# Graph attention on one core: keys in 32-partition transfers, and another order of the first loads

## The chip, the cores and the metric

The kernel runs on one core of a Trainium2 chip. The metric is the device time of one execution in microseconds (us). Three runs before the change took 10,980.81 to 10,985.29 us, with a median of 10,982.34 us.

The core has five engines that run side by side, each with its own list of instructions: TensorE (PE; its weight loads are shown as PEld), VectorE (DVE), ScalarE (ACT), GpSimd (POOL) and SyncE (SP). SP and POOL here issue the data transfers (DMA), which 16 DMA engines carry out. The engines wait for one another, and for transfers, by semaphores.

## The reference

The network has four graph layers over 3,327 nodes with 128 features, all with the same dense 3,327 x 3,327 matrix `adj`. Layer 0 is attention and takes nearly all of the time:

```python
q = (x @ Wq.T).reshape(d, n, h)
k = (x @ Wk.T).reshape(d, n, h)
v = (x @ Wv.T).reshape(d, n, h)
a = jnp.einsum('dnh,dmh->dnm', q, k) * scale
a = a + spatial_encoding + edge_encoding
a = jax.nn.softmax(a, axis=2)
out = jnp.einsum('dnm,dmh->dnh', a, v)
out = out.reshape(n, h * d)
return out @ Wo.T
```

Both encodings are `adj`, `d` is 128 and `h` is 8. So there are 128 "heads" of 8 elements each, and for each head a 3,327 x 3,327 matrix of scores, to which 2 adj is added. Layers 1 to 3 multiply `adj` (and once its transpose) with 3,327 x 128 matrices, with small functions of each row between them.

## The kernel before

**Stages.** A first stage (up to about 419 us in the profile) makes q, k and v, writes them to DRAM in a form cut into a high and a low half (`qS_d`, `kS_d`), and makes the first part of the transposed adj (`adjT`) and a bound for each column's scores. The attention loop follows, and then layers 1 to 3 (from about 10,167 us).

**The attention loop.** It runs over 7 chunks `c` of 476 query columns, in each over 32 groups `g` of 4 heads, and in each group over 13 pairs `q` of key tiles (2 x 128 keys): 224 groups, 2,912 pairs. For a pair, VectorE seeds a PSUM bank with adj minus the bound (`seed`, L645). TensorE then adds the scores of head 0, then those of head 1 minus those of head 0, and so on, four times into the same bank (`scores`, L654), and ScalarE takes the exponential after each (`exps`, L666 and L669; some by VectorE, `hand_exp`, L691 to L697). TensorE multiplies the exponentials with the values into one bank (`values`, L713). At the end of a group VectorE copies that bank out (`store`, L721) and POOL issues four transfers to `oT_d` (L725).

**Tiles that the change touches.** `KT[b]` holds a group's keys, [128 partitions, 3 slots, 1664]. `b` alternates from group to group, so one group's keys can be loaded while the group before computes. Partitions 0 to 63 hold even key tiles (`r` = 0), 64 to 127 odd ones. A score matmul contracts over 64 partitions: 32 for one head and 32 for the head before it, with negative q. The 32 partitions of one head hold its 16 rows of keys (8 elements, high and low half) twice. Head `j` stands in slots `max(0, j-1)` to `j` (heads 0 and 3 in one slot, 1 and 2 in two) at partition `r0 = 64 * r + 32 * (1 - j % 2)`. `QS[b]` holds the group's q the same way, [128, 4, 476]; `QZ[b]` is a second q of head 1 with zeros, for the pairs done in part by VectorE. `VA[b]` holds the values, spread from the loaded `VR` by POOL (`spread_v`, L580).

**How keys and q are loaded.** `load_k` (L551) issues, for each head, each `r` and each of the two copies, a transfer of 16 rows into 16 partitions and one or two slots: 16 transfers a group. `load_q` issues, for each `r`, one transfer of 16 rows (L562) and two of 8 rows (L564, the halves exchanged). `negate_q` (L570, POOL) writes minus slot `j` over all 128 partitions of slot `j + 1`, after which `load_q` of head `j + 1` overwrites its own 32 partitions of each half. So the loads and negations of a group form a ladder: q of head 0, negation, q of head 1, negation, q of head 2, negation, q of head 3. `all_here` (L584, POOL) copies three columns of `KT` to `seen`; the first score matmul of a group waits for it, and so for all keys.

**What sets the order.** The instructions are recorded by hand: the function `loads(u)` puts the next group's loads behind fixed pairs of the present one: keys, q of head 0 and V behind pair 1, a negation and the next q behind pairs 3, 5 and 7, spreading V and `all_here` behind pair 8. All these transfers are issued by SP, whose list is carried out in order. SP uses eight completion semaphores in turn, so a transfer also waits until the one eight places before it has landed. Adj tiles of the next chunk (`load_adj`, L590) and rows of adj for the next part of `adjT` (`Square`, L283) stand in the same list.

**The first group** has no group before it. Its loads are written out ahead of the loop:

```python
v0 = load_v(0, 0)
load_k(0, 0)
load_q(0, 0, 0)
shift_of[0] = load_shift(0)
for j in range(3):
    negate_q(0, 0, j)
    load_q(0, 0, j + 1)
spread_v(0, 0, v0)
here[0] = all_here(0, 0)
adj_of[0] = [load_adj(0, t) for t in range(NT)]
```

Of the kernel before, what the change touches and what calls it, by code (L numbers as in the profile page):

```python
# [10 lines left out]
F32 = mybir.dt.float32  # L11
# [6 lines left out]
ALU = mybir.AluOpType  # L18
# [4 lines left out]
P = 128  # L23
N = 3327
D = 128
H = 8
HD = D * H
NT = 26
NP = NT * P
NQ = NT // 2  # L30

KW = NP // 4
HEADS = D
# [3 lines left out]
CW = 476  # L37
# [40 lines left out]
def width_of(c):  # L78

    return min(CW, N + 1 - c * CW)  # L80
# [8 lines left out]
def gnn_kernel(ctx: ExitStack, tc: tile.TileContext, x, adj, Wq, Wk, Wv, Wo, embed, layer,  # L89
               embed_bias, layer_bias, weight, bias, W_in, W_out, out):  # L90
    nc = tc.nc
# [14 lines left out]
    kS_d = dram.tile([2, H, HEADS, NP], F32, name="kS_d")  # L106
# [219 lines left out]
    with tc.tile_pool(name="a1", bufs=1) as a1, tc.tile_pool(name="a2", bufs=2) as a2, \  # L326
# [23 lines left out]
        for t0 in range(0, NT, 2):  # L350
            for s in "kq":
# [3 lines left out]
                for i in range(2):  # L355
                    t = t0 + i
# [16 lines left out]
                for half in range(2) if s == "q" else ():  # L373
                    nc.sync.dma_start(places(qS_d, t0, 2, H, half * H * GP), st[half].bitcast(F32))
                nc.gpsimd.dma_start(bass.AP(tensor=n2_d[s].tensor, offset=n2_d[s].offset + t0 * P,
                                            ap=[[NT * P, P], [1, 2 * P]]), n2.rearrange("p t i -> p (t i)"))
# [63 lines left out]
    with tc.tile_pool(name="d1", bufs=1) as d1, tc.tile_pool(name="d2", bufs=2) as d2, \  # L440
# [17 lines left out]
        with tc.If(loose > 0):  # L458
# [28 lines left out]
            for c in range(NC):  # L487
# [5 lines left out]
                with tc.For_i(0, HEADS, 1) as d:  # L493
# [6 lines left out]
                        tensor=v_d.tensor, offset=v_d.offset,  # L500
                        ap=[[N * H, HEADS], [NT * H, P], [1, NT * H]])[ds(d, 1)].rearrange("a p x -> (a p) x"))
# [23 lines left out]
    with tc.tile_pool(name="e1", bufs=1) as e1, tc.tile_pool(name="e_adj", bufs=28) as e_adj, \  # L525
# [5 lines left out]
        KT = [e1.tile([P, 3, NQ * P], F32R, name=f"KT{i}") for i in range(2)]  # L531
        QS = [e1.tile([P, 4, CW], F32R, name=f"QS{i}") for i in range(2)]
# [8 lines left out]
        def load_k(c, g):  # L541

            b = (c * NG + g) % 2
            for j in range(4):
                d = 4 * g + j
                k0, nk = max(0, j - 1), 1 if j in (0, 3) else 2
                for r in range(2):
                    r0 = 64 * r + 32 * (1 - j % 2)
                    k_d = kS_d[:, :, d, r * NQ * P:(r + 1) * NQ * P].rearrange("i e n -> (i e) n")
                    for i in range(2):  # L550
                        nc.sync.dma_start(KT[b][r0 + 16 * i:r0 + 16 * i + 16, k0:k0 + nk, :].bitcast(F32),  # L551
                                          k_d.unsqueeze(1).to_broadcast([16, nk, NQ * P]))

        def load_q(c, g, j):

            b = (c * NG + g) % 2
            w, c0, d = width_of(c), c * CW, 4 * g + j
            q_d = qS_d[:, :, d * N + c0:d * N + c0 + w].rearrange("i e n -> (i e) n")
            for r in range(2):
                r0 = 64 * r + 32 * (1 - j % 2)  # L560
                for q_s in [QS[b][:, j, :]] + [QZ[b]] * ((r, j) == (1, 1)):
                    nc.sync.dma_start(q_s[r0:r0 + 16, :w].bitcast(F32), q_d)  # L562
                    for i in range(2):
                        nc.sync.dma_start(q_s[r0 + 16 + 8 * i:r0 + 24 + 8 * i, :w].bitcast(F32),  # L564
                                          q_d[8 - 8 * i:16 - 8 * i])

        def negate_q(c, g, j):

            b, w = (c * NG + g) % 2, width_of(c)
            nc.gpsimd.tensor_scalar(QS[b][:, j + 1, :w], QS[b][:, j, :w].bitcast(F32),  # L570
                                    -1.0, 0.0, op0=ALU.mult, op1=ALU.add)

        def load_v(c, g):
            v = e2.tile([P, 4, NT * H], F32, name="VR", bufs=1)
            nc.sync.dma_start(v, bass.AP(tensor=v_d.tensor, offset=v_d.offset + 4 * g * N * H,
                                         ap=[[NT * H, P], [N * H, 4], [1, NT * H]]))
            return v

        def spread_v(c, g, v):
            nc.gpsimd.tensor_copy(VA[(c * NG + g) % 2][:, :, :, 0:H], v.rearrange("p j (t e) -> p t j e", e=H))  # L580

        def all_here(c, g):

            return nc.gpsimd.tensor_copy(seen, KT[(c * NG + g) % 2][:, :, 0].bitcast(F32))  # L584

        def load_adj(c, t):

            a = e_adj.tile([P, CW], F32, name="a")
            w, c0 = width_of(c), c * CW
            nc.sync.dma_start(a[:, :w], by_tile[t, :, c0:c0 + w])  # L590
            return a

        def load_shift(c):
            w = width_of(c)
            s = e2.tile([P, CW], F32, name="shb", bufs=2)
            nc.sync.dma_start(s[:, :w], bound_d[c * CW:c * CW + w].unsqueeze(0).to_broadcast([P, w]))
            return s

        with tc.If(loose < 1), tc.manual_schedule():
# [12 lines left out]
            n = len(pairs)  # L612
            adj_of, shift_of, v_of, e_of, here = {}, {}, {}, {}, {}
# [113 lines left out]
            def loads(u):  # L727

                c, g, q = pairs[u]
                k = c * NG + g  # L730
                if k + 1 < NC * NG:
                    nxt = divmod(k + 1, NG)
                    if q == 1:
                        load_k(*nxt)
                        load_q(*nxt, 0)
                        v_of[k + 1] = load_v(*nxt)
                    if q in (3, 5, 7):
                        negate_q(*nxt, q // 2 - 1)
                        load_q(*nxt, q // 2)
                    if q == 8:  # L740
                        spread_v(*nxt, v_of.pop(k + 1))
                        here[k + 1] = all_here(*nxt)
                if c + 1 < NC and (g, q) == (0, 0):
                    plan_squares(c)
                if g == NG - 1 and c + 1 < NC:
                    if q == 0:
                        shift_of[c + 1] = load_shift(c + 1)
                        adj_of[c + 1] = []
                    while len(adj_of[c + 1]) < min(NT, 2 * q + 6):
                        adj_of[c + 1].append(load_adj(c + 1, len(adj_of[c + 1])))  # L750
# [4 lines left out]
            def plan(u, f, *a):  # L755
                behind.setdefault(u, []).append((f, a))

            def plan_squares(c):
                for k, s in enumerate(range(squares_of(c), squares_of(c + 1))):
# [7 lines left out]
                    for k, f in ((0, sq.gather), (1, sq.back), (7, sq.finish), (8, sq.store)):  # L767
                        plan(u + k, f)

            v0 = load_v(0, 0)  # L770
            load_k(0, 0)
            load_q(0, 0, 0)
            shift_of[0] = load_shift(0)
            for j in range(3):
                negate_q(0, 0, j)
                load_q(0, 0, j + 1)
            spread_v(0, 0, v0)
            here[0] = all_here(0, 0)
            adj_of[0] = [load_adj(0, t) for t in range(NT)]

            for c in range(NC):
                for q in BY_HAND:
# [7 lines left out]
            def in_slot(i):  # L790

                j = -i % 4
                return (i - 3 * j) // 4, j


            for i in range(-4, 4 * n + 15):
                u, j = in_slot(i)
# [21 lines left out]
                if at % 2:  # L819
                    for k in (1, 2):  # L820
                        u, j = in_slot(i + k)
                        if 0 <= u < n:
                            scores(u, j)
                    u, r = ((i - 11) // 4, 0) if at == 3 else ((i - 13) // 4, 1)
# [682 lines left out]
```

## Time and profile before

| | |
|---|---|
| median of three runs | 10,982.34 us |
| profiled execution, its own time | 10,981.96 us |
| its span, first to last instruction | 10,980.2 us |
| mean granted TensorE clock | 0.985 |
| PE busy | 10,533.5 us, 96% |
| ACT busy | 10,033.1 us, 91% |
| DVE busy | 8,487.1 us, 77% |
| POOL busy | 1,529.1 us, 14% |
| moved by DMA | 1,256.98 MB, mean 114 GB/s |
| share of the transfers issued by SP (queue q1) | 55.7% of 16 engines' span |
| first and last score matmul (L654) | 461.1 and 10,166.9 us |

Busy time is that of each engine. Engines overlap, so shares don't add up. In an order of time a line has the start, the duration, the engine, the line of the kernel, the operation and its tiles; "SPq" is SP's issuing of transfers, and its duration is that of the issue, waits between issues included where several are merged, not of the transfer. In brackets stands the idle time before it and what ended it. In a table of stretches each row has a stretch, its length, each engine's busy time with its number of instructions, the granted clock, the share of the 16 DMA engines' time and GB/s.

### The profile page before, as it was taken

To read this page: it belongs to the slowest core of one execution; us is meant where nothing else is said; L and a number is where in the kernel's file an instruction comes from. 1 tells how busy PE (TensorE), PEld (TensorE's weight loads), DVE (VectorE), ACT (ScalarE), POOL (GpSimd) and SP (SyncE) were. 2 spreads that over 40 slices of the span, in tenths; PEclk is the share of its full clock that TensorE was granted. 3 is DMA by queue.
4 is the path that set the end of the run, shared out by engine and by line. 5 is a ranking of instruction groups with operands and counts; after the bars stand their busy time and mean duration, and the time that the engine had idled before them with its cause. 6 is when DMAs were issued, how large, how long until landed. Compare 5 with 4: busy or idle time off the path is not lost. (4 is left out here: it accounts for less than half of the span.)

```text
span 10980.2 us, 204474 instructions
## 1 busy us (share of the span) xinstructions
PE 10533.5 (96%) x72876; PEld 3435.7 (31%) x72876; DVE 8487.1 (77%) x13503; ACT 10033.1 (91%) x13789; POOL 1529.1 (14%) x2477
## 2 busy tenths in 40 slices
PE   4599999999999999999999999999999999999889
PEld 2133333333333333333333333333323333333544
DVE  5588887888878887788887888878877777777655
ACT  3599999999999999999999999999999999999330
POOL 5011111111111111111111111111111111111101
PEclk7799999999999999999999999999999999999999
DMA  8766566565566565565556565565556555554668
GB/s 250 250 99 97 94 96 113 93 98 96 89 118 97 93 97 88 106 98 97 90 95 119 94 96 93 95 119 95 87 93 98 96 95 86 82 88 71 206 233 281
DMA packets 695339, 1256.98 MB, mean 114 GB/s; under 512 B 195218, under 2 KB 555049, under 8 KB 691244
## 3 DMA queue, kind: packets, MB, share of 16 engines
q1 hardware_dynamic: 644044, 1114.42, 55.7%
q0 software_dynamic: 50272, 129.37, 4.3%
q8 instruction: 587, 9.62, 0.4%
q14 instruction: 436, 3.57, 0.2%
HBM read 1096.53 MB, written 146.60 MB: 113 GB/s over the span
## 5 line engine op out<-in xcount | busy, mean ns | idle before, releaser
L666 ACT ACTIVATE e<-S 128x952 f32<-128x952 f32 (+1 forms) x9024 | 8357.9, 1099 | 36.7 <-PE S L654 29.4
L713 PE MATMUL po<-e,VA 128*9 128x476 f32 (+1 forms) x46592 | 5737.5, 564 | 33.0 <-DVE OS L721 12.3
L645 DVE TENSOR_TENSOR S<-a,shb 128x476 f32<-128x476 f32 (+1 forms) x5824 | 3937.9, 676 | 1447.6 <-ACT e L666 1059.4
L654 PE MATMUL S<-QS,KT 64*128 64x476 f32 (+1 forms) x22176 | 4528.6, 445 | 79.7 <-DMA a<-adjT 28.4
L654 PEld LDWEIGHTS S<-QS,KT 64*128 64x128 f32 x22176 | 2073.7, 184 | 5100.5 <-issue 1301.3
L669 ACT ACTIVATE e<-S 128x476 f32<-128x476 f32 (+1 forms) x4128 | 2467.5, 711 | 1.1 <-PE S L654 0.6
L695 DVE SCALAR_TENSOR_TENSOR e<-e,h 128x476 f32<-128x476 f32 (+1 forms) x2240 | 1497.8, 669 | 77.0
L713 PEld LDWEIGHTS po<-e,VA 128*9 128x9 f32 x46592 | 691.0, 88 | 1606.6 <-issue 1488.1
L570 POOL TENSOR_SCALAR QS<-QS 128x476 fp32r<-128x476 f32 (+1 forms) x672 | 485.6, 723 | 4312.1 <-DMA QS<-qS_d 2612.2
L725 POOL DMA_DIRECT2D oT_d<-OS x896 | 470.5, 530 | 3668.8 <-DVE OS L721 3625.5
L691 DVE TENSOR_SCALAR h<-S 128x476 f32<-128x476 f32 (+1 forms) x1120 | 728.0, 650 | 300.9 <-PE S L654 296.5
L697 DVE SCALAR_TENSOR_TENSOR e<-e,EA 128x476 f32<-128x476 f32 (+1 forms) x1120 | 759.6, 678 | 0.0
L695 DVE SCALAR_TENSOR_TENSOR e<-h 128x476 f32<-128x476 f32 (+1 forms) x1120 | 743.1, 663 | 0.0
L1107 PE MATMUL pu<-strip,y 128*128 128x512 f32 (+2 forms) x1456 | 600.5, 566 | 31.7 <-DVE y L968 14.8
L654 PE MATMUL S<-QZ,KT 64*128 64x476 f32 (+1 forms) x1120 | 493.4, 441 | 11.9 <-DVE S L645 10.5
L1107 PEld LDWEIGHTS pu<-strip,y 128*128 128x128 f32 (+1 forms) x1456 | 271.9, 191 | 305.8 <-issue 272.1
L1111 DVE TENSOR_REDUCE deg<-strip 128x1 f32<-128x1536 f32 (+1 forms) x104 | 193.8, 1881 | 63.7 <-DMA strip<-adjT 44.1
L580 POOL COPY VA<-VR 128x832 f32<-128x832 f32 x224 | 242.3, 1082 | 0.0
L654 PEld LDWEIGHTS S<-QZ,KT 64*128 64x128 f32 x1120 | 205.1, 183 | 92.2 <-DVE S L645 52.4
L288 DVE STREAM_TRANSPOSE cols<-rows 128x416 f32<-128x416 f32 x208 | 204.5, 988 | 30.3 <-DMA rows<-in_adj_dram 22.6
L1060 ACT COPY uT<-pu 128x512 f32<-128x512 f32 (+1 forms) x21 | 11.1, 555 | 222.6 <-PE pu L1107 222.6
L721 DVE COPY OS<-po 128x476 f32<-128x476 f32 (+1 forms) x224 | 146.3, 653 | 87.3 <-PE po L713 87.3
(255 smaller groups left out, 1958.6 us busy)
## 6 DMA issues: line engine op xcount, KB each, us to landing
KT<-kS_d SPq DMA_DIRECT2D x1792, 208.0 KB
KT<-kS_d SPq DMA_DIRECT2D x1792, 104.0 KB
VR<-v_d SPq DMA_DIRECT2D x224, 416.0 KB
QS<-qS_d SPq DMA_DIRECT2D x3072, 14.9 KB
QS<-qS_d SPq DMA_DIRECT2D x1536, 29.8 KB
adjT<-cols SPq DMA_DIRECT2D x26, 1664.0 KB
a<-adjT SPq DMA_DIRECT2D x156, 238.0 KB
strip<-adjT POOLq DMA_DIRECT2D x39, 895.5 KB, 5.1
```

Source lines behind the costliest of these rows:

```text
L570: nc.gpsimd.tensor_scalar(QS[b][:, j + 1, :w], QS[b][:, j, :w].bitcast(F32), -1.0, 0.0, op0=ALU.mult, op1=ALU.add)
L580: nc.gpsimd.tensor_copy(VA[(c * NG + g) % 2][:, :, :, 0:H], v.rearrange("p j (t e) -> p t j e", e=H))
L645: touch(u, [r], nc.vector.tensor_tensor(bank(u, r), adj_of[c][2 * q + r][:, :w], shift_of[c][:, :w], op=ALU.subtract))
L654: x = nc.tensor.matmul(bank(u, r), KT[b][64 * r:64 * r + 64, max(0, j - 1), q * P:(q + 1) * P], q_s[64 * r:64 * r + 64, :w], start=hand an ...
L666: touch(u, (0, 1), nc.scalar.activation(e[:, :, :w], S[:, odd:even + 1, :w], AF.Exp, scale=2.0))
L669: touch(u, [r], nc.scalar.activation(e[:, 1 - r, :w], bank(u, r), AF.Exp, scale=2.0))
L691: touch(u, [1], nc.vector.tensor_scalar(s, bank(u, 1), EXP_ARG, None, op0=ALU.mult))
L695: nc.vector.scalar_tensor_tensor(e, s if k == 3 else e, EXP_C[k], s, op0=ALU.add, op1=ALU.mult)
L697: nc.vector.scalar_tensor_tensor(e, e, EXP_C[0], EA[pairs[u][2]][:, :w], op0=ALU.add, op1=ALU.mult)
L713: nc.tensor.matmul(po[32 * j:32 * j + H + 1, :w], VA[k % 2][:, 2 * pairs[v][2] + of, j, :], e_of[v, j][:, 1 - of, :w], start=(q == 0 and r ...
L725: nc.gpsimd.dma_start(oT_d[:, d * N + c * CW:d * N + c * CW + w], o[32 * j:32 * j + H + 1, :w])
L1107: nc.tensor.matmul(ps[:, :k], y[:m, t, :], s[:m, c * 4 * P - c0:c * 4 * P - c0 + k], start=(t == 0), stop=(t == NT - 1))
```

## The change

`load_k` issues for each head, each `r` and each slot one transfer of 32 partitions: both copies at once, but a slot at a time. The source's access pattern has four levels: two copies (step 0), two halves, 8 elements, 1,664 numbers. The program that is built from it merges halves and elements: the source counts 2, 16 and 1,664, the destination 32 partitions and 1,664. A group has 12 transfers of 208 KB instead of 8 of 208 and 8 of 104; the bytes are the same. This holds for all 224 groups.

The first group's loads are put in another order: q of all four heads, the shift, four adj tiles, then keys, V and the other 22 adj tiles. The three negations over 128 partitions become six over 32 partitions each, of the rows that a score matmul needs, so that they no longer overwrite what the next q load writes, and all q loads can be issued at once. Later groups keep `negate_q` and their order.

```diff
@@ load_k
                 for r in range(2):
                     r0 = 64 * r + 32 * (1 - j % 2)
-                    k_d = kS_d[:, :, d, r * NQ * P:(r + 1) * NQ * P].rearrange("i e n -> (i e) n")
-                    for i in range(2):
-                        nc.sync.dma_start(KT[b][r0 + 16 * i:r0 + 16 * i + 16, k0:k0 + nk, :].bitcast(F32),
-                                          k_d.unsqueeze(1).to_broadcast([16, nk, NQ * P]))
+                    for k in range(k0, k0 + nk):
+                        nc.sync.dma_start(KT[b][r0:r0 + 32, k, :].bitcast(F32), bass.AP(
+                            tensor=kS_d.tensor, offset=kS_d.offset + d * NP + r * NQ * P,
+                            ap=[[0, 2], [H * HEADS * NP, 2], [HEADS * NP, 8], [1, NQ * P]]))
@@ ahead of the loop
+            for j in range(4):
+                load_q(0, 0, j)
+            shift_of[0] = load_shift(0)
+            adj_of[0] = [load_adj(0, t) for t in range(4)]
+            load_k(0, 0)
             v0 = load_v(0, 0)
-            load_k(0, 0)
-            load_q(0, 0, 0)
-            shift_of[0] = load_shift(0)
+            adj_of[0] += [load_adj(0, t) for t in range(4, NT)]
             for j in range(3):
-                negate_q(0, 0, j)
-                load_q(0, 0, j + 1)
+                for r0 in (32 * (1 - j % 2), 64 + 32 * (1 - j % 2)):
+                    nc.gpsimd.tensor_scalar(QS[0][r0:r0 + 32, j + 1, :CW], QS[0][r0:r0 + 32, j, :CW].bitcast(F32),
+                                            -1.0, 0.0, op0=ALU.mult, op1=ALU.add)
             spread_v(0, 0, v0)
             here[0] = all_here(0, 0)
-            adj_of[0] = [load_adj(0, t) for t in range(NT)]
```

## The prediction

> **What bounds the kernel now.** I read the page first, then the order of time around the start of the attention loop, then stretches of 2 us while keys are loaded, then the waits of SP.
>
> ```profile
> PE 10533.5 (96%) x72876; PEld 3435.7 (31%) x72876; DVE 8487.1 (77%) x13503; ACT 10033.1 (91%) x13789; POOL 1529.1 (14%) x2477
> ...
> DMA packets 695339, 1256.98 MB, mean 114 GB/s; under 512 B 195218, under 2 KB 555049, under 8 KB 691244
> ...
> KT<-kS_d SPq DMA_DIRECT2D x1792, 208.0 KB
> KT<-kS_d SPq DMA_DIRECT2D x1792, 104.0 KB
> ```
>
> PE and ACT are full in every slice but the first and the last; DMA is not the bound. The score matmuls of L654 start at 461.1 us and end at 10166.9 us: 9,705.8 us for 224 groups, 43.3 us each. One group needs 2,496 KB of keys (8 transfers of 208 KB and 8 of 104 KB), 2.556 MB.
>
> The start, in order of time, SP and POOL:
>
> ```profile
> 420.26 16.77 SPq L551 DMA_DIRECT2D KT<-kS_d  x16
> 438.46 0.31 SPq L562 DMA_DIRECT2D QS<-qS_d  x1
> ...
> 443.03 0.65 SPq L564 DMA_DIRECT2D QS<-qS_d  x2
> 445.21 0.58 POOL L570 TENSOR_SCALAR QS<-QS 128x476 fp32r<-128x476 f32 x1 [24.32 <-DMA QS<-qS_d]
> 449.36 0.58 POOL L570 TENSOR_SCALAR QS<-QS 128x476 fp32r<-128x476 f32 x1 [3.57 <-DMA QS<-qS_d]
> 453.59 0.59 POOL L570 TENSOR_SCALAR QS<-QS 128x476 fp32r<-128x476 f32 x1 [3.66 <-DMA QS<-qS_d]
> 454.13 0.88 POOL L580 COPY VA<-VR 128x832 f32<-128x832 f32 x1
> 454.95 0.18 POOL L584 COPY seen<-KT 128x3 f32<-128x3 f32 x1
> 455.62 0.65 SPq L564 DMA_DIRECT2D QS<-qS_d  x2
> 456.31 15.14 SPq L590 DMA_DIRECT2D a<-adjT  x26
> ```
>
> Keys first, then a ladder of q load, negation, q load that takes 445.21 to 456.3, and only then adj. Every later group goes down the same ladder, hidden behind 43.3 us of compute. Two stretches while keys move and one while adj moves (the last three columns are granted clock, share of 16 DMA engines, GB/s):
>
> ```profile
> 428.00:430.00 2.00, 2.00 (x4) 0.95 (x3) 0.00 (x0) 0.00 (x0) 0.00 (x0) 0.50 0.99 120
> 5020.00:5022.00 2.00, 2.00 (x18) 0.75 (x21) 1.48 (x3) 2.00 (x4) 0.00 (x0) 1.00 0.95 110
> 468.00:470.00 2.00, 1.80 (x7) 0.79 (x5) 1.97 (x4) 2.00 (x4) 0.00 (x0) 0.50 1.05 401
> ```
>
> All 16 engines are busy in all three, but a 16-partition key transfer gets 110 to 120 GB/s and a 128-partition adj tile 401. So 16 engines that write into few partitions hold each other up (7.5 GB/s each against 25.1). An engine alone is faster: the shortest records of a 6,656-byte key row in the trace are 251 to 253 ns (26.3 GB/s), the median under crowding 765 ns.
>
> **How many engines a transfer uses.** The 195,218 packets under 512 B are nearly all 4-byte ones. Row maxima and bounds (L299, L304, L310) account for 29,952. The rest are completion marks, 165,266. With 16 marks for each of 11,957 issues there would be 191,312. The 4,032 q transfers of 8 rows (14.8 and 14.9 KB in the list of issues), at 8 marks instead of 16, take away 32,256; 7 idle marks for each of POOL's 896 nine-row stores give back 6,272: 165,328, right to 0.1%. So a transfer from SP runs on as many engines as its outermost count can be dealt out to: 8 rows, 8 engines. Before, keys have 16 rows on both sides. After, the tile side counts 32 rows, but the source list is [0,2] copies outermost, then 16 rows. Pieces that are equal on both lists can only be two. I take 2 engines; no transfer of before has such a list, so 16 stays possible.
>
> [...]
>
> **Part by part.** Times are against the profiled execution's own 10,981.96 us (span 10,980.2 and 1.8 around it); the median of the runs is 10,982.34, 0.4 above.
>
> *Keys on two engines.* 12 transfers of 32 rows a group, 192 rows an engine. Bounds from rows: 192 x 0.253 = 48.6 us alone, 192 x 0.765 = 146.9 us if crowded as now, and about 10 us if 16 engines were used (rival 1). Two engines write different halves of 32 partitions and are not crowded, so I take the near end, between 48.6 and the 51.0 that 401/16 GB/s gives: 49.5 us. That alone is over 43.3, so the cover is gone.
>
> *What stands behind the keys.* SP issues in order: keys, q of head 0, V; then the next q waits for POOL's negation. The 6 q transfers of head 0 leave rows on the same two engines behind the keys: 0.5 us. Landing to negation 1.5 us (443.68 to 445.21). The ladder from the first negation to the last q issue 11.1 us (445.21 to 456.3). Only then can SP issue the next group's keys, 1.0 us to first data (an estimate from V's issue at 419.75 and traffic from 420 on). Release of the key buffer is no further wait: the first three transfers overwrite keys of heads 0 and 1, last read before the stalled matmul, and 12 us of data cover the rest. Jobs of some groups stand in the same queue: 88 x 1.7 us for row loads and 136 us in all waiting for row maxima (SP's waits), 1.3 a group. Sum: 49.5 + 0.5 + 1.5 + 11.1 + 1.0 + 1.3 = 64.9, say 65 us a group instead of 43.3. PE idles about 20 us of each; its clock at resumption (0.50 until some 20 us after 461) makes a group's compute perhaps 53 us, still under 65.
>
> 222 such groups: 222 x 21.7 = +4,817 us.
>
> *The start.* 27 q issues from 419.7 at 0.35 us, shift 0.4, four adj tiles at 0.58 (15.14/26): keys are issued at 431.9, data from 433 to 482.5. V 1.3 us behind on those engines, VA copy 0.88, seen 0.18: first scores at 485, not 461 (+24). The ladder of the first group is gone, and its negations cost nothing beside the key load: 6 of 32 partitions instead of 3 of 128, each between 0.18 (the tiny copy) and 0.58; I take 0.5, so +1.3 us on an idle POOL, which would be the price without that cover. 22 adj tiles behind V put 13 us on each engine (8 rows of 1,904 bytes at 25.8 GB/s are 0.59 us a tile), so group 1's keys run from 496 to 545.5, plus 2.0 and 9.9 (445.21 to 455.13): it starts at 557 instead of 504. +53 us. The last group at a low clock at first: +5.
>
> Sum: 4,817 + 53 + 5 = +4,875; 10,982 + 4,875 = 15,857, I say 15,860.
>
> *Issues.* Keys 16 to 12 a group, at 0.37 us: 1.5 us less on SP's queue, nothing on the path. The new form may be issued more slowly; at double that, 4 us beside 49 us of data.
>
> **Rivals.**
> 1. *Not slower: the split goes by the tile's 32 rows.* 16 engines write into twice the partitions, so the load at best halves from its 20 us (420 to 440) to about 10. In the loop it was hidden anyway: SP's wait for keys costs PE nothing, only the POOL copy "seen" gates it, 37.7 us in all:
>
> ```profile
>   PEld S L654: 37.7, 11
> ```
>
> So only the start moves: keys from 433 to 444, V 2, copies 1: first scores at 447, 14 earlier; 10,968 us, -0.13%. For it: the destination is one list of 32, and one 208 KB transfer is nothing unusual. Against: the count of marks. It decides from 4 engines on: 2.556 MB at 4 x 25.8 is 24.8 us, with 15.4 behind it 40, under 43.3; at 3 it is 48.
> 2. *Two engines, but the ladder hides.* If key issues ran ahead of it, the two engines would be the bound: 48.6 + q 2.1 + V 1.3 + adj and rows 1.4 = 53.4 a group; 10,982 + 222 x 10.1 + 58 = 13,280. Against: one queue in order, with q waiting for a negation that waits for data behind the keys.
> 3. *Two engines as slow as today's crowd,* 765 ns a row: 146.9 + 15.4 = 162 a group, 37,500 us. Against: the 251 ns records, and 401 GB/s on many partitions.
>
> **How the numbers follow.** Forecast 0.80, rival 1 0.12, rival 2 0.05, rival 3 0.03. What a measurement can tell from no change is about 0.2%. Rival 1 is mostly within it (0.10 same, 0.02 faster); all others are slower, 0.88. Within the forecast the group lies between 58.5 (rows at 253 ns, ladder 3 us shorter, queue jobs hidden) and 74 (rows at 300 ns as in mixed traffic): 10,982 + 222 x 15.2 + 58 = 14,414 and 17,855. Range 14,300 to 17,900; it leaves out the rivals, 0.20.
>
> **What would show it.** Keys 2688 issues of 208 KB. In the loop, stretches of about 50 us at an eighth of the DMA share and some 50 GB/s, SP's queue waiting for KT landings, and POOL's negations waiting about 40 us each group for q behind keys. PE near 65 to 70% busy with a period of 65 us a group, PEclk below 9 in many slices, and "seen" or a KT landing as what ends the wait before the first score matmul of each group. First scores near 485 us. If instead key stretches show a share near 1.0 and 200 GB/s or more, and PE stays at 96%, rival 1 holds. A period of 53 speaks for 2, of 160 for 3. If the two engines are only slower or faster a row than 0.26 us, the mechanism stands and the term of 49.5 was off.

## The result, and the profile after

The changed kernel takes 16,759.62 us (median of four runs, 16,755.78 to 16,763.79); the kernel before took 10,983.82 us beside it (10,980.81 to 10,989.71). The ratio is 1.526, with a 95% interval of 1.524 to 1.528. The prediction said 15,860 and a range of 14,300 to 17,900: right in sign and mechanism, 900 us too low. The profiled execution of the changed kernel has a span of 16,754.0 us and a mean granted clock of 0.82.

The page of the changed kernel: busy time of the engines, granted clock and DMA share in 40 slices, packets, two groups of instructions, and the list of issues.

```profile
PE 10980.2 (66%) x72876; PEld 3537.1 (21%) x72876; DVE 8339.3 (50%) x13503; ACT 10109.6 (60%) x13789; POOL 1327.0 (8%) x2480
...
PEclk7787888888888888888888888888888888888899
DMA  8222212221122111122212212222221121111167
...
DMA packets 643363, 1256.70 MB, mean 75 GB/s; under 512 B 143250, under 2 KB 503081, under 8 KB 639276
...
L654 PE MATMUL S<-QS,KT 64*128 64x476 f32 (+1 forms) x22176 | 4721.1, 462 | 5414.7 <-POOL seen L584 5137.6
...
KT<-kS_d SPq DMA_DIRECT2D x2688, 208.0 KB
```

The work on each engine is about what it was: PE is busy for 10,980.2 us against 10,533.5 and ACT for 10,109.6 against 10,033.1. What is new is that PE stands still before the score matmuls for 5,414.7 us, nearly all of it until `seen` is written, that is until a group's keys and values are there. The DMA engines are less busy than before, not more: the transfers issued by SP (queue q1) take 21.5% of 16 engines' span instead of 55.7%.

Read as completion marks, one from each engine that takes part in a transfer, the small packets count the engines. Before there were 195,218 under 512 B, now 143,250: 51,968 fewer. That is exactly 3,584 old key transfers with 16 marks each, less 2,688 new ones with 2 each (57,344 - 5,376). By this count the new transfers run on two engines.

Three stretches inside one group's key load in the changed kernel. The columns are stretch, length, busy time and number of instructions of PE, PEld, DVE, ACT and POOL, then granted clock, share of the 16 DMA engines, GB/s:

```profile
8008.00:8013.00 5.00, 5.00 (x44) 1.50 (x36) 2.78 (x5) 5.00 (x8) 0.00 (x0) 1.00 0.13 54
8028.00:8033.00 5.00, 5.00 (x40) 1.59 (x36) 4.09 (x7) 5.00 (x9) 0.00 (x0) 1.00 0.13 53
8043.00:8048.00 5.00, 0.00 (x0) 0.00 (x0) 0.00 (x0) 0.00 (x0) 0.00 (x0) 0.50 0.16 55
```

A share of 0.13 of the DMA engines' time, about an eighth (0.16 in the last stretch), and 53 to 55 GB/s: where the trace before shows 110 to 120 GB/s on 16 engines, there are now two at some 27 each. In the last stretch the group before is finished and nothing computes; the clock is down to 0.50.

One group's loads in order of time, SP and then POOL, in the changed kernel:

```profile
569.50 28.72 SPq L550 DMA_DIRECT2D KT<-kS_d  x12
598.26 3.76 SPq L562 DMA_DIRECT2D QS<-qS_d  x1
...
617.78 0.40 SPq L575 DMA_DIRECT2D VR<-v_d  x1
...
635.62 1.71 SPq L283 DMA_DIRECT2D rows<-in_adj_dram  x4
637.42 7.82 SPq L550 DMA_DIRECT2D KT<-kS_d  x7
...
624.13 0.58 POOL L570 TENSOR_SCALAR QS<-QS 128x476 fp32r<-128x476 f32 x1 [42.91 <-DMA QS<-qS_d]
628.53 0.58 POOL L570 TENSOR_SCALAR QS<-QS 128x476 fp32r<-128x476 f32 x1 [3.81 <-DMA QS<-qS_d]
632.85 0.59 POOL L570 TENSOR_SCALAR QS<-QS 128x476 fp32r<-128x476 f32 x1 [3.73 <-DMA QS<-qS_d]
633.38 0.88 POOL L580 COPY VA<-VR 128x832 f32<-128x832 f32 x1
634.20 0.19 POOL L584 COPY seen<-KT 128x3 f32<-128x3 f32 x1
```

Keys are issued from 569.50, the first negation can start at 624.13 when q has landed behind them, the ladder of negations and q loads takes until after 634.87, and the next keys are issued at 637.42: a period of 67.9 us, 54.6 of it until the first negation and 13.3 behind it. Nothing of this chain overlaps with itself, and the compute of a group is shorter than it.

Who waited for `seen` in the changed kernel, by the view of that tile (engine, tile, line; us in all, times); before it was 37.7 us in 11:

```profile
  PEld S L654: 5384.3, 218
  PE S L654: 5137.6, 217
```

### The profile page after: what moved, and what is told of

It reads as the page before. It is cut to its first block, busy times and chain, and to the rows that moved or that the text cites. A ratio compares the mean times of both kernels' runs of the same rounds, so it can differ in the third digit from the quotient of the medians.

```text
span 16754.0 us, 203351 instructions
## 1 busy us (share of the span) xinstructions
PE 10980.2 (66%) x72876; PEld 3537.1 (21%) x72876; DVE 8339.3 (50%) x13503; ACT 10109.6 (60%) x13789; POOL 1327.0 (8%) x2480
## 2 busy tenths in 40 slices
DMA packets 643363, 1256.70 MB, mean 75 GB/s; under 512 B 143250, under 2 KB 503081, under 8 KB 639276
## 3 DMA queue, kind: packets, MB, share of 16 engines
q1 hardware_dynamic: 592076, 1114.22, 21.5%
## 5 line engine op out<-in xcount | busy, mean ns | idle before, releaser
L654 PE MATMUL S<-QS,KT 64*128 64x476 f32 (+1 forms) x22176 | 4721.1, 462 | 5414.7 <-POOL seen L584 5137.6
L713 PE MATMUL po<-e,VA 128*9 128x476 f32 (+1 forms) x46592 | 6014.6, 590 | 33.2 <-DVE OS L721 11.2
L669 ACT ACTIVATE e<-S 128x476 f32<-128x476 f32 (+1 forms) x4128 | 2419.8, 693 | 5200.3 <-PE S L654 5200.1
L645 DVE TENSOR_TENSOR S<-a,shb 128x476 f32<-128x476 f32 (+1 forms) x5824 | 3852.0, 661 | 1878.6 <-ACT e L666 1413.4
L654 PEld LDWEIGHTS S<-QS,KT 64*128 64x128 f32 x22176 | 2195.1, 193 | 10654.1 <-POOL seen L584 5384.3
L570 POOL TENSOR_SCALAR QS<-QS 128x476 fp32r<-128x476 f32 (+1 forms) x669 | 392.9, 587 | 11406.6 <-DMA QS<-qS_d 11393.9
L697 DVE SCALAR_TENSOR_TENSOR e<-e,EA 128x476 f32<-128x476 f32 (+1 forms) x1120 | 725.0, 647 | 0.0
L654 PE MATMUL S<-QZ,KT 64*128 64x476 f32 (+1 forms) x1120 | 533.0, 476 | 1.7 <-DVE S L645 1.7
L288 DVE STREAM_TRANSPOSE cols<-rows 128x416 f32<-128x416 f32 x208 | 204.6, 989 | 23.8 <-DMA rows<-in_adj_dram 15.9
L580 POOL COPY VA<-VR 128x832 f32<-128x832 f32 x224 | 198.1, 884 | 59.1 <-DMA VR<-v_d 59.1
L1063 ACT COPY uT<-pu 128x512 f32<-128x512 f32 (+1 forms) x21 | 11.1, 553 | 221.6 <-PE pu L1110 221.6
```

What stands on the lines that cost most here:

```text
L288: nc.vector.transpose(self.cols[:, t0:t0 + NQ, 32 * j:32 * j + 32], self.rows.rearrange("p (x t) -> p t x", t=NT)[:, t0:t0 + NQ, :])
L645: touch(u, [r], nc.vector.tensor_tensor(bank(u, r), adj_of[c][2 * q + r][:, :w], shift_of[c][:, :w], op=ALU.subtract))
L654: x = nc.tensor.matmul(bank(u, r), KT[b][64 * r:64 * r + 64, max(0, j - 1), q * P:(q + 1) * P], q_s[64 * r:64 * r + 64, :w], start=hand an ...
L669: touch(u, [r], nc.scalar.activation(e[:, 1 - r, :w], bank(u, r), AF.Exp, scale=2.0))
L697: nc.vector.scalar_tensor_tensor(e, e, EXP_C[0], EA[pairs[u][2]][:, :w], op0=ALU.add, op1=ALU.mult)
L713: nc.tensor.matmul(po[32 * j:32 * j + H + 1, :w], VA[k % 2][:, 2 * pairs[v][2] + of, j, :], e_of[v, j][:, 1 - of, :w], start=(q == 0 and r ...
```

## The experiments

The question was not only whether the keys are the cause, but which property of their transfers, and what part the rest of the loop has in it. In the tables and sums, "load" is the time from the start of a group's first 6,656-byte key row to the end of its last (median over the groups) and "period" the mean time from one group to the next.

### One part at a time: keys alone, order alone

The first kernel is the one before with only the new `load_k`; the second is the changed kernel with only the old `load_k`, that is, with the new order alone.

```diff
@@ load_k (keys alone: this edit in the kernel before; order alone: its reverse in the changed kernel)
-                    for i in range(2):
-                        nc.sync.dma_start(KT[b][r0 + 16 * i:r0 + 16 * i + 16, k0:k0 + nk, :].bitcast(F32),
-                                          k_d.unsqueeze(1).to_broadcast([16, nk, NQ * P]))
+                    for k in range(k0, k0 + nk):
+                        nc.sync.dma_start(KT[b][r0:r0 + 32, k, :].bitcast(F32), bass.AP(...
+                            ap=[[0, 2], [H * HEADS * NP, 2], [HEADS * NP, 8], [1, NQ * P]]))
```

Expected of the keys alone:

> The kernel before with the new key transfers alone; the first group's loads stay in their old order. Theory (two engines carry the keys, the loop's 222 groups pay): 16,700 to 16,800 us, the same 69 us a group as with both edits. Rival (the new order of the first loads takes part in the loss, for instance because adj tiles and q now collide with keys): clearly under 16,700 us.

Measured: 16,767.37 us, ratio 1.526 (1.524 to 1.528), load 51.3, period 69.1. The whole loss is that of the key transfers.

Expected of the order alone:

> The changed kernel with the old 16-partition key transfers: the new order of the first loads alone. Theory: first scores some 5 us earlier than 461 us, since the ladder is gone and keys move at their old 120 GB/s; 10,970 to 10,985 us, no measurable difference. Rival (the order costs as such): 11,000 us or more.

Measured: 10,976.76 us, ratio 0.9994 (0.9985 to 1.0003). The first scores come 4.5 us earlier (456.7 against 461.2), which is 0.04% of the time and cannot be told from no change. With the old keys the order of the first loads gains next to nothing; with the new ones it costs next to nothing (16,767.37 without it, 16,759.62 with it).

### The same 32 partitions with 16 rows outermost

Is it the 32 partitions of the destination, or the two copies at the head of the source's list? Here a transfer still fills 32 partitions, but the list runs over 16 rows first and over the copies inside. The copies of a row then lie in neighbouring partitions, and q is loaded in the same pattern so that rows still meet.

```diff
-                            ap=[[0, 2], [H * HEADS * NP, 2], [HEADS * NP, 8], [1, NQ * P]]))
+                            ap=[[HEADS * NP, 16], [0, 2], [1, NQ * P]]))
@@ load_q
-                    nc.sync.dma_start(q_s[r0:r0 + 16, :w].bitcast(F32), q_d)
+                    nc.sync.dma_start(q_s[r0:r0 + 32:2, :w].bitcast(F32), q_d)
                     for i in range(2):
-                        nc.sync.dma_start(q_s[r0 + 16 + 8 * i:r0 + 24 + 8 * i, :w].bitcast(F32),
+                        nc.sync.dma_start(q_s[r0 + 1 + 16 * i:r0 + 16 + 16 * i:2, :w].bitcast(F32),
```

> The changed kernel, with the two copies moved inward: the source counts 16 rows, then 2 copies, so a row's copies stand in neighbouring partitions, and q is loaded to match. Still one transfer of 32 partitions and 208 KB, 12 a group, each row read twice. Theory (the outermost count sets the engines): 16 engines, key load 10 to 13 us instead of 51, first scores near 447 to 450 us, 10,960 to 10,985 us. Rival (32 partitions in a transfer, or the repeated row as such, is what is slow): 16,000 us or more.

Measured: 10,997.61 us, ratio 1.0011 (1.0002 to 1.0020). The packets under 512 B and two stretches during a key load in this kernel:

```profile
DMA packets 680995, 1256.85 MB, mean 114 GB/s; under 512 B 180882, under 2 KB 540713, under 8 KB 676908
```

```profile
8014.00:8016.00 2.00, 2.00 (x18) 0.68 (x14) 1.93 (x4) 2.00 (x4) 0.00 (x0) 1.00 0.82 220
8018.00:8020.00 2.00, 2.00 (x18) 0.72 (x21) 1.42 (x4) 2.00 (x4) 0.00 (x0) 1.00 0.99 216
```

180,882 is 195,218 less 3,584 x 16 plus 2,688 x 16, exactly: 16 engines a transfer. The share is 0.82 and 0.99, the rate over 200 GB/s, and a group's keys come in 12.1 us instead of 51.3. So 32 partitions in a transfer are not the cause.

The gain at the start that was expected here did not come: first scores at 460.6, not at 447 to 450, and the time is 13 us above the range. The order of time of SP in this kernel says why:

```profile
424.28 0.53 SPq L562 DMA_DIRECT2D QS<-qS_d  x1
424.86 1.32 SPq L564 DMA_DIRECT2D QS<-qS_d  x2
...
440.28 1.85 SPq L590 DMA_DIRECT2D a<-adjT  x4
442.17 3.28 SPq L550 DMA_DIRECT2D KT<-kS_d  x5
```

A q transfer to every second partition is issued in 0.53 us, two of the 8-row ones in 1.32, against 0.32 and 0.65 in the kernel with the order alone; 27 of them take some 8 us longer and put the keys 9 us later (442.17 against 433.32 there). And it was V, not the keys, that the values' copy waited for until 459.49. In the loop a group takes 43.28 us instead of 43.15 in the median, from one `store` to the next (43.36 instead of 43.29 in the mean); what makes up that tenth of a microsecond was not settled.

### A count of two without copies

The other half of the question: is it the step of 0 that leaves a transfer two engines, or the count of 2? Here a transfer has no step of 0 at all. One unused row is put between the high and the low half of `kS_d`, so that halves and elements cannot be merged any more, and the kernel before is left with transfers of 16 partitions whose source counts 2, 8 and 1,664.

```diff
-    kS_d = dram.tile([2, H, HEADS, NP], F32, name="kS_d")
+    kS_d = dram.tile([2, H + 1, HEADS, NP], F32, name="kS_d")[:, 0:H]
@@ load_k
-                    k_d = kS_d[:, :, d, r * NQ * P:(r + 1) * NQ * P].rearrange("i e n -> (i e) n")
-                    for i in range(2):
-                        nc.sync.dma_start(KT[b][r0 + 16 * i:r0 + 16 * i + 16, k0:k0 + nk, :].bitcast(F32),
-                                          k_d.unsqueeze(1).to_broadcast([16, nk, NQ * P]))
+                    k_d = kS_d[:, :, d, r * NQ * P:(r + 1) * NQ * P]
+                    for k in range(k0, k0 + nk):
+                        for i in range(2):
+                            nc.sync.dma_start(KT[b][r0 + 16 * i:r0 + 16 * i + 16, k, :].bitcast(F32), k_d)
```

> The kernel before, with the key array in DRAM padded between its high and low half, so that the 16 rows of a transfer count 2, then 8; 16 partitions, one slot a transfer (24 of 104 KB a group), no repeated row and no step of 0 anywhere. Theory (a count of 2 outermost leaves two engines, whatever its step): 192 rows an engine as in the changed kernel, 16,600 to 16,900 us. Rival (the step of 0 in the source, or reading a row twice, is the cause): 10,980 to 11,050 us.

Measured: 16,542.19 us, ratio 1.506 (1.504 to 1.508), load 50.4, period 68.1. That is 58 us below the range expected: a key row takes 261 ns in the mean here and 266 in the changed kernel; why was not settled. The page of this kernel, and one stretch in a key load:

```profile
DMA packets 648760, 1256.89 MB, mean 76 GB/s; under 512 B 148626, under 2 KB 508457, under 8 KB 644652
...
KT<-kS_d SPq DMA_DIRECT2D x5376, 104.0 KB
```

```profile
8000.00:8010.00 10.00, 10.00 (x76) 3.10 (x72) 7.10 (x12) 10.00 (x15) 0.00 (x0) 1.00 0.13 54
```

148,626 is 195,218 - 3,584 x 16 + 5,376 x 2, exactly. Neither the copies nor the 32 partitions are needed for the loss: a source that counts 2 outermost, with rows of its own behind both counts, ran on two engines at 54 GB/s too.

### Half of the keys on two engines

How much slower may the keys become before it shows? One kernel takes the new transfers for heads 1 and 2 (8 of the 12), the other for heads 0 and 3 (4 of the 12); the other heads keep the old ones.

```diff
@@ load_k (heads 1 and 2 new; for heads 0 and 3 new the condition is j not in (0, 3))
+                    if j not in (1, 2):
+                        k_d = kS_d[:, :, d, r * NQ * P:(r + 1) * NQ * P].rearrange("i e n -> (i e) n")
+                        for i in range(2):
+                            nc.sync.dma_start(KT[b][r0 + 16 * i:r0 + 16 * i + 16, k0:k0 + nk, :].bitcast(F32),
+                                              k_d.unsqueeze(1).to_broadcast([16, nk, NQ * P]))
+                        continue
```

> The changed kernel, with the new transfers for heads 1 and 2 alone (8 of 12) and the old 16-partition transfers for heads 0 and 3. Theory (time follows the rows that two engines carry): 128 rows at 0.267 us and 8 of the old ones, some 36 us, plus the 16.8 us that stand around a key load: 53 us a group, 12,700 to 13,600 us. Rival (a fixed price for having such transfers at all): near the changed kernel, 16,000 us or more.

> As in the run with heads 1 and 2, but the new transfers for heads 0 and 3 alone (4 of 12). Theory: 64 rows at 0.267 us plus 16 rows of crowded old transfers make a load of 26 to 29 us; with 16.8 us around it 43 to 46 us a group, just where it begins to show over 43.3 us of compute: 10,980 to 11,600 us. Rival (price in proportion to the transfers, with no threshold): 4 of 12 of the loss of 5,776 us, 12,900 us.

Measured: 14,009.51 us for heads 1 and 2 (ratio 1.275, 1.273 to 1.277) and 12,624.28 us for heads 0 and 3 (1.149, 1.147 to 1.151). Both are above the ranges expected, the second by 1,000 us and nearer to its rival. The loads explain it:

| kernel | load, us | period, us | difference, us |
|---|---|---|---|
| rows outermost | 12.1 | 43.3 | hidden |
| old keys, new order | 19.8 | 43.3 | hidden |
| before | 20.1 | 43.3 | hidden |
| new keys for heads 0 and 3 | 32.8 | 50.6 | 17.8 |
| new keys for heads 1 and 2 | 39.3 | 56.7 | 17.4 |
| halves apart | 50.4 | 68.1 | 17.7 |
| after | 51.3 | 69.0 | 17.7 |
| new keys alone | 51.3 | 69.1 | 17.8 |

The mixed loads were priced too low (32.8 us where 26 to 29 were expected, 39.3 where 36 were), and what stands around a load is 17.4 to 17.8 where 16.8 was taken. In the five kernels whose load shows, the period is the load plus about 17.7. By extrapolation, a load shows from 43.3 - 17.7 = 25.6 us on, which would leave the kernel before 5.5 us to spare, a quarter of its load. This is an estimate: the runs bracket the bound only between 20.1 and 32.8 us.

### Without the ladder

In the changed kernel all four heads' q are loaded right behind the keys, in every group, and the negations, over 32 partitions, come at the old places without a q load behind them. If the ladder alone keeps the next keys back, this should end near the second rival's time.

```diff
@@ negate_q
-            nc.gpsimd.tensor_scalar(QS[b][:, j + 1, :w], QS[b][:, j, :w].bitcast(F32),
-                                    -1.0, 0.0, op0=ALU.mult, op1=ALU.add)
+            for r0 in (32 * (1 - j % 2), 64 + 32 * (1 - j % 2)):
+                nc.gpsimd.tensor_scalar(QS[b][r0:r0 + 32, j + 1, :w], QS[b][r0:r0 + 32, j, :w].bitcast(F32),
+                                        -1.0, 0.0, op0=ALU.mult, op1=ALU.add)
@@ pair 1
                         load_k(*nxt)
-                        load_q(*nxt, 0)
+                        for j in range(4):
+                            load_q(*nxt, j)
@@ pairs 3, 5, 7
                         negate_q(*nxt, q // 2 - 1)
-                        load_q(*nxt, q // 2)
```

> The changed kernel, keys still on two engines, but every group loads its q as the first group does: all four heads' q right behind the keys, and the negations over 32 partitions each, so that no q load waits for a negation. Theory (a group lasts as long as its key load plus what SP can only do behind it, here the ladder of 11 to 13 us): the next keys start right behind q and V, a group takes 53 to 55 us instead of 69, 13,100 to 13,700 us. Rival (the two engines alone set the group's time, and the ladder is hidden): above 16,300 us.

Measured: 15,636.18 us, ratio 1.423 (1.421 to 1.426), load 50.5, period 64.0: 5 us a group gained, where the expectation had 13.8 to 16.5 ((16,760 - 13,700)/222 to (16,760 - 13,100)/222). The time lies between theory and rival, and neither holds as it was put. The order of time of this kernel, SP and then POOL, at the end of a load:

```profile
8029.35 0.32 SPq L562 DMA_DIRECT2D QS<-qS_d  x1
8033.44 0.61 SPq L564 DMA_DIRECT2D QS<-qS_d  x2
8034.10 0.32 SPq L562 DMA_DIRECT2D QS<-qS_d  x1
...
8039.72 0.97 SPq L564 DMA_DIRECT2D QS<-qS_d  x2
8040.79 0.39 SPq L576 DMA_DIRECT2D VR<-v_d  x1
8041.29 2.02 SPq L550 DMA_DIRECT2D KT<-kS_d  x3
...
8034.16 1.25 POOL L571 TENSOR_SCALAR QS<-QS 32x476 fp32r<-32x476 f32 x2 [46.15 <-DMA QS<-qS_d]
...
8045.23 0.19 POOL L585 COPY seen<-KT 128x3 f32<-128x3 f32 x1
```

The waits on POOL are gone from SP's list, but SP uses eight completion semaphores in turn, and a q issue waits until the key transfer that holds its semaphore has landed: the view of SP's waits in this kernel puts 3,853.5 us in 1,115 waits of q issues (L562 and L564) down to landings of keys. Until 8,033 the q transfers are let in one every 4 us, as keys land; the other 21 q and V issues then take until 8,041.18, after the keys, and the next keys stand behind them. The time between first negation and the issue of the next keys falls from 13.7 to 9.4 us only (means over the groups). That the next keys wait for work that SP can do only behind the present ones is borne out; but the ladder of negations is only 4.3 of those 13.7 us.

### Old keys without the ladder

The same edits with the old keys, and then only the split negations, both in the kernel with the new order alone, to see what the ladder costs where the keys are hidden. The edit is the one above; the second kernel takes its first part (`negate_q`) alone.

> The kernel before's key transfers on 16 engines, the new order of the first loads, and no ladder in any group (all q at once, negations over 32 partitions). Theory (a ladder hidden behind 43.3 us of compute costs nothing): the same as the order alone, 10,965 to 10,990 us. Rival (the ladder costs something in the loop even when hidden, as POOL time or as a late start of the next group): 10,940 us or less; or slower, 11,000 us or more, since POOL has 6 negations a group instead of 3.

> As the run with the old keys and no ladder, but with the ladder back in the loop: old key transfers, new order of the first loads, q loaded head by head at the old places, and only the negations split into 32 partitions each, 6 a group instead of 3. It tells apart why that run was 129 us slower than before. Theory now (a 32-partition negation takes POOL as long as a 128-partition one, and POOL's added 2.2 us a group slow VectorE beside it): 11,050 to 11,130 us. Rival (q loaded all at once behind the keys is what costs): 10,965 to 10,995 us.

Measured: 11,112.99 us without the ladder (ratio 1.0117, 1.0100 to 1.0134) and 11,099.60 us with split negations alone (1.0102, 1.0085 to 1.0119). The first is slower, as one of its rivals had it; the second is in its range. So nearly all of the loss, 112 of 129 us, is that of six negations instead of three, not of q loaded at once. Stretch 500 to 10,000 us, groups of instructions by line (busy us, mean ns of one; idle before), first of the kernel before:

```profile
L645 DVE TENSOR_TENSOR S<-a,shb 128x476 f32<-128x476 f32 (+1 forms) x5704 | 3857.7, 676 | 1410.8 <-ACT e L666 1031.7 <-ACT e L669 126.2 <-DVE S L645 6.2
```

```profile
L570 POOL TENSOR_SCALAR QS<-QS 128x476 fp32r<-128x476 f32 (+1 forms) x658 | 476.0, 723 | 4186.5 <-DMA QS<-qS_d 2532.4 <-PE S L654 1332.9 <-PE po L713 285.4
```

and of the kernel with split negations:

```profile
L646 DVE TENSOR_TENSOR S<-a,shb 128x476 f32<-128x476 f32 (+1 forms) x5630 | 3894.5, 692 | 1254.7 <-ACT e L667 894.4 <-ACT e L670 106.6 <-DVE S L646 5.9
```

```profile
L571 POOL TENSOR_SCALAR QS<-QS 32x476 fp32r<-32x476 f32 (+1 forms) x1296 | 1010.9, 780 | 2889.0 <-DMA QS<-qS_d 1875.7 <-PE S L655 811.9 <-PE po L714 124.1
```

A negation over 32 partitions was no shorter than one over 128 (780 ns against 723), so twice as many double POOL's time for them, from 476 to 1,011 us, and VectorE's seeds are then 692 ns long instead of 676. The time is 112 us over the 10,987.37 of the kernel before beside it. That VectorE's longer seeds are what costs them is argued from these rows, not isolated. One more row agrees that the seeds go with POOL's negations: in the second kernel of the next section, where POOL has none, they take 666 ns over the same stretch.

### Negations on VectorE

Three kernels, all with the old keys, looked for a place for the negations on VectorE, where one takes 0.40 us (medians of 399 to 402 ns). The first (new order, ladder kept) issues them from VectorE at pairs 3, 5 and 7; the second (no ladder, split) puts two each at pairs 9, 10 and 11; the third (ladder kept, 128 partitions) puts them at pairs 9, 11 and 12 with their q loads behind them.

```diff
@@ first
-            nc.gpsimd.tensor_scalar(QS[b][:, j + 1, :w], QS[b][:, j, :w].bitcast(F32),
+            nc.vector.tensor_scalar(QS[b][:, j + 1, :w], QS[b][:, j, :w].bitcast(F32),
@@ second: nc.vector for the split negations, and
-                    if q in (3, 5, 7):
-                        negate_q(*nxt, q // 2 - 1)
+                    if q in (9, 10, 11):
+                        negate_q(*nxt, q - 9)
@@ third: the first, and
-                    if q in (3, 5, 7):
-                        negate_q(*nxt, q // 2 - 1)
-                        load_q(*nxt, q // 2)
+                    if q in (9, 11, 12):
+                        negate_q(*nxt, (9, 11, 12).index(q))
+                        load_q(*nxt, (9, 11, 12).index(q) + 1)
```

> The old key transfers, the new order of the first loads, and the loop's three negations a group moved from POOL to VectorE (over 128 partitions, at the same places). If POOL's work beside VectorE is what three more negations cost 112 us for, three fewer should give back part of it: theory 10,890 to 10,970 us, since VectorE has 20% idle time and takes 3 instructions of at most 0.65 us for POOL's 3 of 0.72 to 0.74. Rival (VectorE, in order, is held by a negation that waits for its q to land, or has no room): 11,000 us or more.

> Old key transfers, new order of the first loads, q of all heads at once behind the keys, and the negations over 32 partitions on VectorE, two each at pairs 9, 10 and 11, when q has long landed. Theory: VectorE is held by nothing now and POOL has no negation left, so it takes back what POOL's negations cost beside VectorE: 10,850 to 10,960 us. Rival (VectorE has no room for six more instructions of 0.4 us a group, 540 us in all): 11,000 us or more.

> The same with three negations over 128 partitions on VectorE and q loaded head by head behind them, at pairs 9, 11 and 12. Theory: 1.2 us of VectorE a group instead of 2.4, so 10,830 to 10,950 us if the ladder's last q still lands in time. Rival (the ladder now ends too late, or VectorE waits for a landing as in the run with negations at pairs 3, 5 and 7): 11,050 us or more.

Measured: 13,891.50 us (ratio 1.264, 1.262 to 1.266), 11,199.31 us (1.020, 1.019 to 1.022) and 11,253.26 us (1.025, 1.024 to 1.027), so all three came out as their rivals had it. The negations' line in the first of the three:

```profile
L570 DVE TENSOR_SCALAR QS<-QS x669: 396/401/410, 487.9 to 13034.5; 128x476 fp32r<-128x476 f32 x144, 128x472 fp32r<-128x472 f32 x24
...
  DMA QS<-qS_d: 2390.6, 223
```

and in the second:

```profile
L571 DVE TENSOR_SCALAR QS<-QS x1338: 385/399/1135, 484.1 to 10333.1; 32x476 fp32r<-32x476 f32 x164, 32x472 fp32r<-32x472 f32 x28
...
  DMA QS<-qS_d: 1.3, 5
```

In the first, VectorE waits 10.7 us a group for q to land, with the seeds that PE needs queued behind the wait. In the second the wait is gone (1.3 us in all) and 219 us are still lost: six times 0.43 us a group on an engine that is 77% busy come through as 1.0 us a group. In the third 521.4 us of waits for q remain. None of the kernels run is measurably faster than the one before; the order alone is nearest.

## Why the prediction came out as it did

**Two engines.** Right, and the point on which all hung. The count of completion marks, from which the prediction read that a transfer runs on as many engines as its outermost count can be dealt out to, is exact in all five forms of the key load that were run beside the old one, the two mixed ones too (170,130 and 168,338 packets under 512 B: 144 and 136 marks a group instead of 256). The first rival had the destination's list decide. A 32-partition destination did get 16 engines (180,882 small packets, 216 to 246 GB/s), but only in the kernel whose source counts 16 rows outermost.

**The terms of a group,** means over the groups of the loop:

| step of the prediction | predicted, us | measured, us |
|---|---|---|
| key load, 192 rows an engine | 49.5 | 51.3 |
| q rows, landing to first negation | 0.5 + 1.5 | 1.9 |
| ladder and other jobs of the queue | 11.1 + 1.3 | 13.7 |
| issue to first key | 1.0 | 2.1 |
| sum, the period | 65 | 69.0 |

Three terms were too short, by 1.8, 1.3 and 1.1 us. The largest miss is the row: 258 ns were taken, between the 253 of a row alone and the 266 that 401 GB/s over 16 engines gives. The median row does take 256 ns, but one in twenty takes over 280, and the mean is 266; 192 x 0.266 = 51.1 of the 51.3 us, so the two engines had next to no gaps. The medians of the other two are 13.1 and 1.5 us; their means are higher because in some groups loads of adj rows stand in the queue ahead of the keys, as at 635.62 us above. Together, 222 x (69.03 - 65) = 895 us, nearly all of the 900 that were missing. The 1.5 us was read as starting at a landing, but 443.68 is the end of an issue; the size came out right all the same. And the ladder's term has about the right size, but not the whole reason: without the ladder, most of that time is still there, since the q transfers wait for completion semaphores instead.

**The range.** With the terms it names, its ends come to 48.6 + 2.0 + 8.1 + 1.0 = 59.7 and 57.6 + 15.4 = 73.0 us a group, not 58.5 and 74; by these the range would be some 14,700 to 17,600 us, and the measured time lies in both.

**The start** was predicted at 485 us for the first scores and came at 492.6. Of the 7.6 us, 3 are the stage before, which ended that much later (first q issue at 422.97, not 419.7), so that the keys were issued at 434.87 instead of 431.9. The first key row came 3.0 us behind that issue instead of 1.1, the load took 51.9 us instead of 49.5, and VA's copy started 1.7 us behind the last key row (491.54 and 489.80), where 1.3 was taken. V's own issue took 3.96 us, from 464.53, against 0.40 in the kernel before; why was not settled (the view of SP's waits has none between 460 and 470 us), but it was over long before the keys were there.

**The release of the key buffer** was costed at nothing. The view of SP's waits puts 1,760.2 us in 890 waits at the key issues down to score matmuls; some of these may be waits for a completion semaphore instead, since an issue waits for both. Either way they pass while earlier key rows are being moved: the key load has no gaps. So a price of nothing is right, with the cover it named.

**The compute of a group at a low clock** was put at 53 us and is 45.2: PE's gaps of over 1.5 us are 5,321 us, 23.8 a group, and 69.0 - 23.8 = 45.2. The prediction took some 20 us at half the clock from the first group; in the group whose scores start at 8,066.92 us the granted clock is 0.67 from 8,068 to 8,072 and 1.00 from there to 8,076. Both figures are below the period, so the error has no price.

**The rivals.** The first, "16 engines, 10,968", did not happen; where 16 engines were made to do it, the load took 12.1 us where it had 10, and the time was 10,997.61, slower by 0.1%. That kernel also issues its q more slowly, so what 16 engines would give with the old q loads was not measured. Its bound, "decides from 4 engines on", was drawn with 15.4 us around the load; with the measured 17.7 the load may take 25.6 us, and four engines would need 24.8 to 25.5 (192/2 rows at 0.258 or 0.266): on the edge, and not tried. The second, "13,280 if the ladder hides", did not happen either. Taking the ladder's waits out of SP's list is not enough for it: the time was still 15,636.18. Its own condition, key issues that run ahead of the q loads, was not tried. The third, crowded rows at 765 ns, did not happen in the changed kernel, but it does in part of a mixed load: with heads 0 and 3 new, the stretch 8,028 to 8,030 us has a DMA share of 1.05 at 114 GB/s, some 0.93 us a row if 16 engines share it (an estimate), and 8,038 to 8,040 us has 0.12 at 50 GB/s, two engines as in the changed kernel. How much of the crowding falls on the new rows was not separated.

## What to carry to other kernels

Before two transfers are merged into one, look at what the new one's source counts outermost: in these kernels a count of 2 there, copies or not, left 2 of 16 engines and made the load 2.5 times as long (51.3 and 50.4 us against 20.1), though the bytes stayed and in the changed kernel issues became fewer. The count of very small packets on the profile's page told how many engines the key transfers used: in the five forms run beside the old one it fits 2 or 16 for each transfer exactly. A load that is hidden is hidden up to a bound, here by estimate load plus 17.7 us against 43.3; in the kernels beyond it every microsecond was paid in every group, and what stands in the same queue behind the load was paid with it.

## What the runs showed of the hardware that was not expected

- A transfer whose source has rows of its own behind both counts of an outermost 2 ran on two engines like a repeated one: 148,626 small packets, 54 GB/s, 16,542.19 us.
- In the stretches named, sixteen engines moved 110 to 120 GB/s with transfers into 16 partitions (before, 428 to 432 and 5,020 to 5,022 us), 216 to 246 into 32 (rows outermost, 8,012 to 8,020) and 401 into 128 (before, 468 to 470); two engines moved 53 to 55 into 32 (after, the three stretches of its key load above). So two engines into 32 partitions had half the rate of sixteen into 16. What makes sixteen engines about twice as fast into 32 partitions as into 16 was not shown.
- The time of an issue went with the form of its transfer: 0.32 us for q into neighbouring partitions, 0.53 into every second one, and no key transfer of the changed kernel took less than 0.61 to issue where the shortest old one took 0.31.
- POOL took as long to negate 32 partitions as 128 (0.58 us each with VectorE idle beside it; 0.78 and 0.72 in the loop), and VectorE's seeds went with POOL's load: over 500 to 10,000 us 662 ns in the changed kernel, where much of POOL's work falls into VectorE's pauses, 666 with no negation on POOL, 676 before, 692 with six negations a group.
